# Graph attention on one Trainium2 core: two heads in the halves of a PSUM bank, weight sums in quarters, chunks of 768 columns

## The chip, the core and the metric

The kernel runs on one core of a Trainium2 chip. The metric is the device time of one execution in microseconds (us), and the median of several runs stands for it. One further execution was taken with the hardware profiler, and the parts of the profile come from that one. The engines are PE (TensorE, matrix products), DVE (VectorE), ACT (ScalarE), POOL (GpSimd) and SP (here it only issues DMAs). PSUM is the memory that PE writes its products to[...].

## What is computed

Two layers run on 2708 nodes with 512 features. The change touches only layer 0, an attention over a graph with eight heads of 64 features:

```python
feats = jnp.einsum('nf,hfd->hnd', X, W)
e_self = jnp.einsum('hnd,hd->hn', feats, a_self)
e_neigh = jnp.einsum('hnd,hd->hn', feats, a_neigh)
dense = e_self[:, :, None] + e_neigh[:, None, :]
dense = jnp.where(dense >= 0, dense, LEAKY_ALPHA * dense)
mask = NEG_INF * (1.0 - A)
attn = jax.nn.softmax(dense + mask[None, :, :], axis=-1)
out = jnp.einsum('hnm,hmd->hnd', attn, feats) + b[:, None, :]
```

Here A is the adjacency matrix of zeros and ones, X the normalised and clipped input. The result goes through a relu and is added to the input. Layer 1 (a diffusion with two steps and a nucleus cut) uses A too, in the form A plus the identity and its row and column sums.

## The kernel before

The exponential of a leaky relu is the larger of two products, so an attention weight, up to a factor of its own row, is max(r, k) times A times exp(e_neigh). The factor r belongs to the attending node, k to the neighbour. So the kernel never forms the softmax: DVE computes e = max(r_b, kk) * a_c in one instruction (line 455), and PE multiplies it with `fw`, the features times exp(e_neigh) (line 457). `fw` holds 65 columns for each head: 64 features, and one column with exp(e_neigh) alone, whose product is the sum of the weights. The division by this sum comes at the end.

All this is done in fp32. The 2708 nodes make 22 row tiles: 21 of 128 rows and one of 20. The neighbours lie on the partitions (index `t`), the attending nodes on the columns. The columns are cut into six chunks, four of 512, one of 384 and one of 276 (`tchunks`, line 213). For each chunk:

- Lines 431 to 444: for every row tile `t`, SP loads the chunk's piece of the transposed adjacency, `a_c` (24 buffers of 512 fp32 columns). ACT copies it to `s_c`, summing as it goes; POOL adds the identity on the diagonal; SP stores it to `s_d` for layer 1.
- Line 446, `row_sums`: SP loads 128 whole rows of the adjacency into `arow` (one buffer) and ACT sums them.
- Line 343, `shares`: r is loaded, the same on all partitions, for four heads at a time (`r_b`).
- Lines 449 to 462: the eight heads come in two groups of four. A group has four PSUM accumulators `po`, one bank each out of six, with 65 partitions used. For each of 22 row tiles and each of four heads there are one DVE product e (ten buffers) and one matmul. After the last row tile ACT copies the four accumulators to `o_t` (line 462).
- `finished` (line 351) gives the last part for each row tile of a finished chunk as five stages: `turned` transposes `o_t` on PE; `shared` divides by the sums; `normed` and `cleared` do layer 1's normalisation; `asked` makes transposes and a projection for layer 1. They are put into `later` and are issued, one stage at a time, between the row tiles of the next chunk's first group. Those of the last chunk are issued after its loop.

The order of the instructions on each engine is the program's order as the tile framework lays it out; waits are made by semaphores from the buffers' readers and writers. Layer 1 begins at line 476 and takes the larger part of the time.

Of the kernel before, what the change touches and what calls it, by code (L numbers as in the profile page):

```python
# [9 lines left out]
F32 = mybir.dt.float32  # L10
# [14 lines left out]
P = 128  # L25
# [28 lines left out]
def kernel(  # L54
# [154 lines left out]
    HG = 4  # L209
    hgroups = [list(range(g, min(g + HG, H))) for g in range(0, H, HG)]  # L210

    NB = -(-NT // TG)
    tchunks = []
    for c in range(NB):
        t0 = tchunks[-1][-1] + 1 if c else 0
        tchunks.append(list(range(t0, t0 + NT // NB + (c < NT % NB))))
    with ExitStack() as l0:
        big = l0.enter_context(tc.tile_pool(name="l0", bufs=1))
        fw = big.tile([P, NT, H, DV], F32, name="fw")
# [114 lines left out]

        def row_sums(t):
            pr = rows[t]
            arow = adjp.tile([P, N], F32, name="arow", bufs=1)
            nc.sync.dma_start(out=arow[:pr], in_=adj[cols[t], :])
            nc.scalar.activation(arow[:pr], arow[:pr], AF.Copy, accum_out=rsum[:pr, t:t + 1])
            nc.gpsimd.tensor_scalar(lone[:pr, t:t + 1], rsum[:pr, t:t + 1], 0.0, None, op0=OP.is_equal)  # L340
            nc.gpsimd.tensor_scalar(lone_n[:pr, t:t + 1], lone[:pr, t:t + 1], float(N), None, op0=OP.mult)

        def shares(grp, n0, cw):
            r_b = rbp.tile([P, HG, 512], F32, name="r_b")
# [6 lines left out]
        def finished(t, o_t, c0, bank, final):  # L351


            pr = rows[t]
            f3 = fsum.rearrange("p (h d) -> p h d", h=H)
            pns, held = [], []

            def turned():
                xt = work.tile([P, D], F32, name="xt0", bufs=3)
                nc.sync.dma_start(out=xt[:pr], in_=x[cols[t], :])  # L360
                held.append(xt)
                for g, grp in enumerate(hgroups):
                    pn = bank(g)
                    pns.append(pn[:, :HG * DV].rearrange("p (h d) -> p h d", h=HG))
                    for i, hd in enumerate(grp):
                        nc.tensor.transpose(pns[g][:pr, i, :], o_t[:, hd, c0:c0 + pr], ident[:DV, :DV])

            def shared():
                den = small.tile([P, H], F32, name="den")
                rden = small.tile([P, H], F32, name="rden")  # L370
                o = work.tile([P, D], F32, name="o", bufs=3)
                held.append(o)
                o3 = o.rearrange("p (h d) -> p h d", h=H)
                for pn, grp in zip(pns, hgroups):
                    nc.vector.tensor_scalar(den[:pr, grp[0]:grp[-1] + 1], pn[:pr, :, DH],
                                            lone_n[:pr, t:t + 1], None, op0=OP.add)
                nc.vector.reciprocal(rden[:pr], den[:pr])
                for pn, grp in zip(pns, hgroups):
                    s = slice(grp[0], grp[-1] + 1)
                    nc.vector.scalar_tensor_tensor(o3[:pr, s, :], f3[:pr, s, :], lone[:pr, t:t + 1],  # L380
                                                   pn[:pr, :, :DH], op0=OP.mult, op1=OP.add)
# [12 lines left out]

            def with_beta(o):
                xt = held[0]
                nc.gpsimd.tensor_add(xt[:pr], o[:pr], beta_b[:pr])
                nc.gpsimd.dma_start(out=xb_d[cols[t], :], in_=xt[:pr])

            def cleared():  # L400
                _, o, mean, rs = held
                v = turn.tile([P, D], F32, name="v")
                held.append(v)
                nc.vector.tensor_scalar(o[:pr], o[:pr], mean, rs, op0=OP.subtract, op1=OP.mult)
                nc.scalar.activation(v[:pr], o[:pr], AF.Relu)
# [20 lines left out]
        for ci, tiles in enumerate(tchunks):  # L426
# [3 lines left out]
            a_c = []  # L430
            for t in range(NT):
                pr = rows[t]
                a_c.append(adjp.tile([P, 512], F32, name="a_c", bufs=NT + 2))
                nc.sync.dma_start(out=a_c[t][:pr, :cw], in_=adj_t[cols[t], n0:n1])
                s_c = small.tile([P, 512], F32R, name="s_c", bufs=4)
                wide = len(tiles) * P
                if pr < P or cw < wide:
                    nc.gpsimd.memset(s_c.bitcast(F32), 0.0)
                nc.scalar.activation(s_c[:pr, :cw], a_c[t][:pr, :cw], AF.Copy,  # L439
                                     accum_out=cpart[:pr, t, ci:ci + 1])  # L440
# [7 lines left out]
            o_t = work.tile([DV, H, 512], F32, name="o_t", bufs=1)  # L448
            for grp, r_b in zip(hgroups, r_bs):
                po = [ps_o.tile([P, 512], F32, name="po")[:DV] for _ in grp]  # L450
                for t in range(NT):
                    pr = rows[t]
                    for i, hd in enumerate(grp):
                        e = tp.tile([P, 512], F32, name="e")
                        nc.vector.scalar_tensor_tensor(e[:pr, :cw], r_b[:pr, i, :cw], kk[:pr, t, hd:hd + 1],  # L455
                                                       a_c[t][:pr, :cw], op0=OP.max, op1=OP.mult)
                        nc.tensor.matmul(po[i][:, :cw], lhsT=fw[:pr, t, hd, :], rhs=e[:pr, :cw],  # L457
                                         start=(t == 0), stop=(t == NT - 1))
                    for stage in later.pop(t, ()):
                        stage()  # L460
                for i, hd in enumerate(grp):
                    nc.scalar.copy(o_t[:, hd, :cw], po[i][:, :cw])

            final = ci == len(tchunks) - 1
            for i, t in enumerate(tiles):
                if final:
                    bank = lambda g: ps_o.tile([P, 512], F32, name="po")
                else:
                    bank = lambda g: ps_t.tile([P, 512], F32, name=f"pn{g}")
                for n, stage in enumerate(finished(t, o_t, t * P - n0, bank, final)):  # L470
# [983 lines left out]
```

## Time and profile before

| what | value |
|---|---|
| median of three runs | 3573.36 us (3570.47 to 3583.9) |
| profiled execution, its own time | 3562.47 us |
| span of the profile | 3560.7 us |
| mean granted clock of PE | 0.976 |
| first and last matmul of line 457 begin | 138.6 us, 1044.2 us |
| PE, DVE, ACT, POOL busy, of the whole span | 94%, 74%, 42%, 25% |

A group line of the profile names the source line, the engine, the operation, what is written and read, the shape and the number of instructions; then the busy time and the mean of one in ns; then the idle time of the engine just before, and what ended it. PEld is PE's loading of the weights, which can run beside the matmuls. Durations of matmuls include the time in the pipeline, so they overlap in the trace; the distance from one weight load to the next shows the real pace. An answer for one line says how long its engine was idle before it, how many times, and until what.

### The profile page before, as it was taken

What the parts mean: (1) busy time and instruction counts of PE and PEld (TensorE: products, weight loads), DVE (VectorE), ACT (ScalarE), POOL (GpSimd) and SP (SyncE); (2) the same over time, 40 slices, a digit from 0 to 9 for tenths busy, and PEclk for the clock granted to TensorE, in tenths of its full rate; (3) what the DMA queues carried; (4) which work ended last, traced back from release to release, by engine and by line L of the source; (5) the groups of instructions that cost most, each with busy time, mean ns of one, the idle gap of its engine ahead of it and who ended that gap; (6) DMA issues with size and microseconds to landing.
All of it is one profiled execution on the core that took longest, in us unless ns stands there. A gap on an engine that the chain in (4) does not pass through costs nothing. (4 is left out here: it accounts for less than half of the span.)

```text
span 3560.7 us, 34129 instructions
## 1 busy us (share of the span) xinstructions
PE 3332.0 (94%) x10797; PEld 1729.1 (49%) x10797; DVE 2650.8 (74%) x4828; ACT 1508.6 (42%) x2269; POOL 890.4 (25%) x1074
## 2 busy tenths in 40 slices
PE   8999999998988999999999999899998999988998
PEld 4433333333455544646555554465555555555554
DVE  4587888889985756545464734598899998888883
ACT  2344211111103676566565642353655554545610
POOL 4114241415321121211222221311312332212211
PEclk9999999999999999999999999999999999999999
DMA  4476424242327624525344453695545535556453
GB/s 116 155 244 243 154 95 139 76 125 84 103 98 269 238 83 153 196 90 208 108 157 170 136 175 101 226 307 169 175 163 189 199 130 183 174 183 210 163 202 124
DMA packets 251348, 579.99 MB, mean 163 GB/s; under 512 B 33945, under 2 KB 76553, under 8 KB 248291
## 3 DMA queue, kind: packets, MB, share of 16 engines
q1 hardware_dynamic: 229063, 503.39, 42.7%
q0 software_dynamic: 22064, 74.09, 5.4%
q8 instruction: 86, 1.41, 0.2%
q14 instruction: 135, 1.11, 0.1%
HBM read 471.68 MB, written 105.68 MB: 162 GB/s over the span
## 5 line engine op out<-in xcount | busy, mean ns | idle before, releaser
L1140 PE MATMUL a<-va,at 128*128 128x512 f32 (+2 forms) x1936 | 887.1, 598 | 5.0 <-ACT at L1122 4.7
L457 PE MATMUL po<-e,fw 128*65 128x512 f32 (+4 forms) x2112 | 841.9, 554 | 28.8 <-DVE e L455 20.4
L455 DVE SCALAR_TENSOR_TENSOR e<-r_b,kk,a_c 128x512 f32<-128x512 f32 (+4 forms) x1056 | 750.4, 739 | 70.0 <-PE po L457 19.0
L576 ACT ACTIVATE junk_a<-p,nth 128x2708 uint8<-128x2708 f32 (+1 forms) x240 | 612.8, 2553 | 32.1 <-POOL nth L591 27.6
L1014 PE MATMUL q<-hl,s_r 128*128 128x512 f32 x1936 | 537.9, 424 | 63.3 <-DMA s_r<-s_d 45.3
L457 PEld LDWEIGHTS po<-e,fw 128*65 128x65 f32 (+1 forms) x2112 | 287.3, 140 | 543.5 <-issue 275.1
L1140 PEld LDWEIGHTS a<-va,at 128*128 128x128 f32 (+2 forms) x1936 | 338.3, 186 | 374.5 <-issue 341.9
L1014 PEld LDWEIGHTS q<-hl,s_r 128*128 128x128 f32 x1936 | 363.5, 192 | 225.9 <-issue 64.8
L1122 ACT COPY at<-t 128x512 f32<-128x512 f32 (+3 forms) x308 | 140.6, 478 | 655.8 <-PE t L1118 652.4
L655 DVE SCALAR_TENSOR_TENSOR junk<-p,th 128x2708 bf16<-128x2708 f32 (+1 forms) x132 | 407.2, 3085 | 3.0
L1034 PE MATMUL q<-u_k,v 128*128 128x512 f32 x704 | 316.9, 592 | 0.8 <-ACT v L1024 0.8
L1017 PE MATMUL q<-s_r,hl 128*128 128x512 f32 (+1 forms) x1056 | 282.3, 413 | 15.2 <-DMA s_r<-s_d 11.1
L1017 PEld LDWEIGHTS q<-s_r,hl 128*128 128x128 f32 x1056 | 196.0, 192 | 94.9 <-issue 51.6
L1034 PEld LDWEIGHTS q<-u_k,v 128*128 128x128 f32 x704 | 133.3, 190 | 158.6 <-issue 154.4
L544 ACT COPY p<-t 128x452 f32<-128x452 f32 (+2 forms) x264 | 131.3, 536 | 162.0 <-PE t L542 115.6
L542 PE MATMUL t<-keys,q_t 128*128 128x452 f32 x528 | 160.9, 432 | 41.2 <-ACT p L544 38.1
L851 DVE MAX8 vn<-keep 128x8 f32<-128x2708 f32 (+1 forms) x66 | 196.8, 2981 | 2.3
L569 DVE TENSOR_REDUCE nmx<-p 128x1 f32<-128x2708 f32 (+1 forms) x44 | 130.5, 2967 | 88.1 <-ACT p L544 88.1
L439 ACT ACTIVATE s_c<-a_c 128x512 fp32r<-128x512 f32 (+3 forms) x132 | 76.2, 577 | 249.0 <-DMA a_c<-in_adj_t_dram 122.3
L1187 PE MATMUL a<-u_k,v_t 128*128 128x512 f32 (+1 forms) x352 | 168.6, 619 | 5.2 <-ACT yo L1194 3.0
L1118 PEld LDWEIGHTS t<-ident,keep 128*128 128x128 f32 (+1 forms) x968 | 114.7, 139 | 76.1 <-issue 46.5
L1118 PE MATMUL t<-ident,keep 128*128 128x128 f32 (+1 forms) x968 | 145.3, 272 | 2.9 <-ACT p L544 2.8
(311 smaller groups left out, 3358.2 us busy)
## 6 DMA issues: line engine op xcount, KB each, us to landing
hl<-vhl_d SPq DMA_DIRECT2D x132, 512.0 KB
s_r<-s_d SPq DMA_DIRECT2D x264, 256.0 KB
hl<-fhl_d SPq DMA_DIRECT2D x132, 512.0 KB
hl<-bhl_d SPq DMA_DIRECT2D x132, 512.0 KB
u_k<-in_L_gnn_U_dram SPq DMA_DIRECT2D x184, 256.0 KB
arow<-in_adj_dram SPq DMA_DIRECT2D x21, 1354.0 KB
s_r<-s_d SPq DMA_DIRECT2D x132, 192.0 KB
s_d<-s_c SPq DMA_DIRECT2D x88, 256.0 KB
```

Source lines behind the costliest of these rows:

```text
L455: nc.vector.scalar_tensor_tensor(e[:pr, :cw], r_b[:pr, i, :cw], kk[:pr, t, hd:hd + 1], a_c[t][:pr, :cw], op0=OP.max, op1=OP.mult)
L457: nc.tensor.matmul(po[i][:, :cw], lhsT=fw[:pr, t, hd, :], rhs=e[:pr, :cw], start=(t == 0), stop=(t == NT - 1))
L542: nc.tensor.matmul(pl[:, :c1 - c0], lhsT=q[:, i], rhs=self.keys[:, c0:c1], start=(i == 0), stop=(i == 1))
L576: nc.scalar.activation(junk[:pr], self.p[i][:pr], func, **kw)
L655: nc.vector.scalar_tensor_tensor(self.junk_b[:pr], p, th, p, op0=OP.is_ge, op1=OP.mult, accum_out=dst)
L851: v.max(vs, keep[0][:pr])
L1014: nc.tensor.matmul(half[j], lhsT=s_r[:, j * P:(j + 1) * P], rhs=hl[:, h], start=(c == 0 and h == 0), stop=(c == NT - 1 and h == 1))
L1017: nc.tensor.matmul(half[j][:, :w], lhsT=hl[:, h, j * P:(j + 1) * P], rhs=s_r[:, :w], start=(c == 0 and h == 0), stop=(c == NT - 1 and h == 1))
L1034: nc.tensor.matmul(half[j], lhsT=across_t[-1][k][:, j * P:(j + 1) * P], rhs=u_k, start=(start and k == 0), stop=(start and k == KD - 1))
L1118: nc.tensor.transpose(pt[:rows[c], j, :pr], keep[i][:pr, cols[c]], ident[:pr, :pr])
L1140: nc.tensor.matmul(pa[:pr], lhsT=at[:rows[c], j, :pr], rhs=va[:rows[c], c, :], start=(c == 0), stop=(c == NT - 1))
L1187: nc.tensor.matmul(pz[i][:rows[t]], lhsT=v_t[i][:, k, :rows[t]], rhs=u_k, start=(k == 0), stop=(k == KD - 1))
```

## The change

The accumulators no longer have 65 partitions. Two heads share one bank: head i of a pair has partitions 0 to 63 or 64 to 127, so each matmul has 64 weight columns. The sums of the weights get banks of their own: four heads in four quarters of 32 partitions, where the one column with exp(e_neigh) is read 32 times (`to_broadcast`). Three kinds of accumulator (two pairs, one of sums) by two parts of at most 512 columns take six banks, so a chunk has 768 columns: three chunks of 768 and one of 404 instead of six. A chunk of 768 is streamed to PE in two parts of 384.

To make room, the adjacency is loaded into `a_f` (three fp32 buffers) and ACT casts it to `a_c` in bf16 (zeros and ones stay exact); `s_c` has three buffers instead of four; `arow` holds half a row; e has six buffers of 768 columns instead of ten of 512. `o_t` holds two heads on its 128 partitions, `o_d` the sums; a row tile then takes six transposes instead of eight. The stages in `later` are placed anew.

```diff
-    NB = -(-NT // TG)
-    tchunks = []
...
+    TC = 6
+    WC = TC * P
+    tchunks = [list(range(t, min(t + TC, NT))) for t in range(0, NT, TC)]
+    NG = len(hgroups)
+    NPR = HG // 2
...
-        tp = l0.enter_context(tc.tile_pool(name="l0t", bufs=10))
+        tp = l0.enter_context(tc.tile_pool(name="l0t", bufs=6))
...
-            arow = adjp.tile([P, N], F32, name="arow", bufs=1)
-            nc.sync.dma_start(out=arow[:pr], in_=adj[cols[t], :])
-            nc.scalar.activation(arow[:pr], arow[:pr], AF.Copy, accum_out=rsum[:pr, t:t + 1])
+            half = small.tile([P, 2], F32, name="half")
+            w = -(-N // 2)
+            for i in range(2):
+                arow = adjp.tile([P, w], F32, name="arow", bufs=1)
+                c = slice(i * w, min((i + 1) * w, N))
+                arow = arow[:pr, :c.stop - c.start]
+                nc.sync.dma_start(out=arow, in_=adj[cols[t], c])
+                nc.scalar.activation(arow, arow, AF.Copy, accum_out=half[:pr, i:i + 1])
+            nc.gpsimd.tensor_tensor(rsum[:pr, t:t + 1], half[:pr, 0:1], half[:pr, 1:2], op=OP.add)
...
-                a_c.append(adjp.tile([P, 512], F32, name="a_c", bufs=NT + 2))
-                nc.sync.dma_start(out=a_c[t][:pr, :cw], in_=adj_t[cols[t], n0:n1])
-                s_c = small.tile([P, 512], F32R, name="s_c", bufs=4)
+                a_f = adjp.tile([P, WC], F32, name="a_f", bufs=3)
+                nc.sync.dma_start(out=a_f[:pr, :cw], in_=adj_t[cols[t], n0:n1])
+                a_c.append(adjp.tile([P, WC], BF16, name="a_c", bufs=NT + 2))
+                nc.scalar.copy(a_c[t][:pr, :cw], a_f[:pr, :cw])
+                s_c = small.tile([P, WC], F32R, name="s_c", bufs=3)
...
-            for grp, r_b in zip(hgroups, r_bs):
-                po = [ps_o.tile([P, 512], F32, name="po")[:DV] for _ in grp]
+            halfs = -(-cw // 512)
+            hw = -(-cw // halfs)
+            parts = [(a, min(a + hw, cw)) for a in range(0, cw, hw)]
+            for gi, (grp, r_b) in enumerate(zip(hgroups, r_bs)):
+                po = [[ps_o.tile([P, 512], F32, name="po") for _ in parts] for _ in range(NPR + 1)]
                 for t in range(NT):
                     pr = rows[t]
-                    for i, hd in enumerate(grp):
-                        e = tp.tile([P, 512], F32, name="e")
-                        nc.vector.scalar_tensor_tensor(e[:pr, :cw], r_b[:pr, i, :cw], kk[:pr, t, hd:hd + 1],
-                                                       a_c[t][:pr, :cw], op0=OP.max, op1=OP.mult)
-                        nc.tensor.matmul(po[i][:, :cw], lhsT=fw[:pr, t, hd, :], rhs=e[:pr, :cw],
-                                         start=(t == 0), stop=(t == NT - 1))
-                    for stage in later.pop(t, ()):
+                    es = []
+                    for k in range(NPR):
+                        for i in (2 * k, 2 * k + 1):
+                            hd = grp[i]
+                            e = tp.tile([P, WC], F32, name="e")
+                            es.append(e)
+                            nc.vector.scalar_tensor_tensor(e[:pr, :cw], r_b[:pr, i, :cw], kk[:pr, t, hd:hd + 1],
+                                                           a_c[t][:pr, :cw], op0=OP.max, op1=OP.mult)
+                        for n, (a, b) in enumerate(parts):
+                            for i in range(2):
+                                nc.tensor.matmul(po[k][n][i * DH:(i + 1) * DH, :b - a],
+                                                 lhsT=fw[:pr, t, grp[2 * k + i], :DH], rhs=es[2 * k + i][:pr, a:b],
+                                                 start=(t == 0), stop=(t == NT - 1))
+                    w = P // HG
+                    for n, (a, b) in enumerate(parts):
+                        for i, hd in enumerate(grp):
+                            nc.tensor.matmul(po[NPR][n][i * w:(i + 1) * w, :b - a],
+                                             lhsT=fw[:pr, t, hd, DH:].to_broadcast([pr, w]), rhs=es[i][:pr, a:b],
+                                             start=(t == 0), stop=(t == NT - 1))
+                    for stage in later.pop(gi * NT + t, ()):
                         stage()
-                for i, hd in enumerate(grp):
-                    nc.scalar.copy(o_t[:, hd, :cw], po[i][:, :cw])
+                for k in range(NPR + 1):
+                    for n, (a, b) in enumerate(parts):
+                        to = o_t[:, gi * NPR + k, a:b] if k < NPR else o_d[:, gi, a:b]
+                        nc.scalar.copy(to, po[k][n][:, :b - a])
...
-                if final:
+                if final and i < 3:
...
-                    later.setdefault(n if final else i * 5 + n, []).append(stage)
+                    later.setdefault(n if final else 3 * i + n + n // 4, []).append(stage)
```

More of the change, by code (lines that the diff above doesn't have):

```diff
@@ L210 @@
     hgroups = [list(range(g, min(g + HG, H))) for g in range(0, H, HG)]
-    NB = -(-NT // TG)
-    tchunks = []
-    for c in range(NB):
-        t0 = tchunks[-1][-1] + 1 if c else 0
-        tchunks.append(list(range(t0, t0 + NT // NB + (c < NT % NB))))
+    TC = 6
[3 more added lines that the diff above has]
+    NPR = HG // 2
     with ExitStack() as l0:
@@ L343, in shares @@
         def shares(grp, n0, cw):
-            r_b = rbp.tile([P, HG, 512], F32, name="r_b")
+            r_b = rbp.tile([P, HG, WC], F32, name="r_b")
             nc.sync.dma_start(
@@ L349, in shares, with finished @@
             return r_b
-        def finished(t, o_t, c0, bank, final):
+        def finished(t, o_t, o_d, c0, bank, final):
             pr = rows[t]
-            f3 = fsum.rearrange("p (h d) -> p h d", h=H)
             pns, held = [], []
@@ L361, in turned @@
                 held.append(xt)
-                for g, grp in enumerate(hgroups):
-                    pn = bank(g)
-                    pns.append(pn[:, :HG * DV].rearrange("p (h d) -> p h d", h=HG))
-                    for i, hd in enumerate(grp):
-                        nc.tensor.transpose(pns[g][:pr, i, :], o_t[:, hd, c0:c0 + pr], ident[:DV, :DV])
+                for g, (src, n) in enumerate(((o_t, H // 2), (o_d, NG))):
+                    pns.append(bank(g).rearrange("p (k d) -> p k d", k=KD))
+                    for k in range(n):
+                        nc.tensor.transpose(pns[g][:pr, k, :], src[:, k, c0:c0 + pr], ident)
             def shared():
@@ L373, in shared @@
                 o3 = o.rearrange("p (h d) -> p h d", h=H)
-                for pn, grp in zip(pns, hgroups):
-                    nc.vector.tensor_scalar(den[:pr, grp[0]:grp[-1] + 1], pn[:pr, :, DH],
-                                            lone_n[:pr, t:t + 1], None, op0=OP.add)
+                pn, pd = pns
+                nc.vector.tensor_scalar(den[:pr], pd[:pr, :NG, ::P // HG].rearrange("p g i -> p (g i)"),
+                                        lone_n[:pr, t:t + 1], None, op0=OP.add)
                 nc.vector.reciprocal(rden[:pr], den[:pr])
[L378 to L381, printed above, removed]
+                nc.vector.scalar_tensor_tensor(o[:pr], fsum[:pr], lone[:pr, t:t + 1],
+                                               pn[:pr].rearrange("p k d -> p (k d)"), op0=OP.mult, op1=OP.add)
                 eng = nc.vector if final else nc.gpsimd
@@ L438 @@
                     nc.gpsimd.memset(s_c.bitcast(F32), 0.0)
-                nc.scalar.activation(s_c[:pr, :cw], a_c[t][:pr, :cw], AF.Copy,
+                nc.scalar.activation(s_c[:pr, :cw], a_f[:pr, :cw], AF.Copy,
                                      accum_out=cpart[:pr, t, ci:ci + 1])
@@ L447 @@
             r_bs += [shares(grp, n0, cw) for grp in hgroups[1:]]
-            o_t = work.tile([DV, H, 512], F32, name="o_t", bufs=1)
-            for grp, r_b in zip(hgroups, r_bs):
-                po = [ps_o.tile([P, 512], F32, name="po")[:DV] for _ in grp]
+            o_t = work.tile([P, H // 2, WC], F32, name="o_t", bufs=1)
+            o_d = work.tile([P, NG, WC], F32, name="o_d", bufs=1)
+            halfs = -(-cw // 512)
+            hw = -(-cw // halfs)
+            parts = [(a, min(a + hw, cw)) for a in range(0, cw, hw)]
@@ L460 @@
+                    w = P // HG
[5 more added lines that the diff above has]
+                    for stage in later.pop(gi * NT + t, ()):
                         stage()
-                for i, hd in enumerate(grp):
-                    nc.scalar.copy(o_t[:, hd, :cw], po[i][:, :cw])
+                for k in range(NPR + 1):
+                    for n, (a, b) in enumerate(parts):
+                        to = o_t[:, gi * NPR + k, a:b] if k < NPR else o_d[:, gi, a:b]
+                        nc.scalar.copy(to, po[k][n][:, :b - a])
@@ L469 @@
                     bank = lambda g: ps_t.tile([P, 512], F32, name=f"pn{g}")
-                for n, stage in enumerate(finished(t, o_t, t * P - n0, bank, final)):
-                    later.setdefault(n if final else i * 5 + n, []).append(stage)
+                for n, stage in enumerate(finished(t, o_t, o_d, t * P - n0, bank, final)):
+                    later.setdefault(n if final else 3 * i + n + n // 4, []).append(stage)
         for n in sorted(later):
```

## The prediction

> **What bounds the kernel now.** The change touches only the graph attention of layer 0, so I first find that stretch. In the page's forty slices PE, the matmul engine, is at 8 or 9 tenths nearly throughout. The table of groups then gives the loop's two instructions, the answer for line 457 and the wait table of the stretch from 138 to 1050 us say who waits for whom:
>
> ```profile
> L457 PE MATMUL po<-e,fw 128*65 128x512 f32 (+4 forms) x2112 | 841.9, 554 | 28.8 <-DVE e L455 20.4
> L455 DVE SCALAR_TENSOR_TENSOR e<-r_b,kk,a_c 128x512 f32<-128x512 f32 (+4 forms) x1056 | 750.4, 739 | 70.0 <-PE po L457 19.0
> ```
> ```profile
>   DVE e L455: 230.9, 636
>   ACT o_t L462: 23.6, 13
> ```
> ```profile
> DVE e L455 <- PE po L457: 19.0, 31, 6.0
> ```
>
> The reader sees 1056 products e on DVE (VectorE) and twice as many matmuls: every fp32 matmul is two instructions. The second fence is the answer for line 457, what PE and its weight loads waited for (us, times): at the ends of groups ACT's copies out of PSUM, 23.6 us in all; the 230.9 on e are mostly loads that arrive early and lie under the matmul before. The third is the wait table: DVE waits for PE 31 times. Line 457 runs from 138.6 to 1044.2 us: 905.6 us. Who sets its pace is read from the timeline of PE's weight loads at the switch from 128 to 20 rows:
>
> ```profile
> 212.37 0.14 PEld L457 LDWEIGHTS po<-e,fw 128*65 128x65 f32 x1 [0.29 <-issue]
> 213.31 0.19 PEld L457 LDWEIGHTS po<-e,fw 20*65 20x65 f32 x2 [0.81 <-DVE e L455]
> 213.80 0.13 PEld L457 LDWEIGHTS po<-e,fw 20*65 20x65 f32 x1 [0.30 <-issue]
> 214.23 0.13 PEld L457 LDWEIGHTS po<-e,fw 20*65 20x65 f32 x1 [0.30 <-issue]
> ```
>
> In steady state a load comes every 0.43 us and hides under the matmul before it: 0.429 us for 512 columns, 0.838 ns a column and instruction. Here the same three loads take 1.43 us instead of 1.29: **a switch of array mode costs 0.14 us**, and its first load is not pulled ahead. Streaming alone is 1408 x 0.429 (512 columns) + 352 x 0.322 (384) + 352 x 0.231 (276) = 798 us, 108 short of the stretch. So PE bounds the stage. DVE is next: the table of six windows, 138 to 1050 us, sums to
>
> ```profile
> sum 912.00, PE 873.84 PEld 327.82 DVE 810.17 ACT 195.66 POOL 270.54; mean PE 145.64 PEld 54.64 DVE 135.03 ACT 32.61 POOL 45.09
> ```
>
> DVE's 810 us are 750 of e and some 60 of the later stages.
>
> **What the Trainium skill says.** "FP8 and Floating Point Precision", TensorE Precision Notes: true fp32 takes four passes. The trace agrees in kind: two instructions for each matmul of line 457; it doesn't show the passes within one. "TensorE: Matmul & The Clock Gate", Part 3: small matmuls in different column strips of the array run at once (three of 32 columns: 2.38x), but matmuls start and end in program order. No matmul of the trace before pairs strips, so it shows neither. "TensorEngine Tiling (Array Packing)", Key Properties: a change of tiling mode drains the array; the 0.14 us above agrees. "VectorE: DVE Perf Modes", What auto-detection actually checks: the two-per-cycle form of a two-input operation wants every tensor 16 bits wide. Only a_c becomes bf16 while r_b and e stay fp32, so I give DVE nothing for the type; no run here shows it.
>
> **The change part by part.**
>
> *DVE.* 1056 products become 704: 528 of 768 columns and 176 of 404. In this stretch the means are 793 ns (512), 700 (384), 567 (276): 0.96 ns a column. So 768 take 793 + 256 x 0.96 = 1.04 us, 404 take 0.69, together 549 + 121 = 670 us, 80 less than now. DVE isn't the bound, so by itself this is worth nothing.
>
> *PE.* For one group of four heads and one row tile of 768 columns, PE now streams 8 x 768 x 0.838 ns = 5.15 us. After, two pairs in halves, two parts of 384 columns: 8 matmuls; the sums in quarters: 8 more. That is 32 instructions of 0.322 us, and two mode switches (64 to 32 columns and back), 0.28. The time depends on what overlaps. I take this rule: a strip's instruction starts when its own strip is free and none ahead of it still waits. Each head's two instructions share a strip, so the second waits for the first and holds up the next head. The halves then overlap two deep (8 slots of 0.322 for 16 instructions, plus one to fill), but the quarters also only two deep: 8 slots plus one. 18 x 0.322 + 0.28 = **6.08 us** against 5.15. For 404 columns (one part): 10 x 0.339 + 0.28 = 3.67. With 2 x 22 x 3 = 132 of the first and 44 of the second: 803 + 161 = **964 us** of streaming, for 798.
>
> *Buffers.* e falls from ten of 512 to six of 768, and all four e of a row tile are held until the sums have read them. DVE can be only two products ahead. Under the rule above e0 is free some 1.3 us before the sums end, so the third and fourth products are ready in time. Where the quarters overlap four deep, it bites (below).
>
> *The rest of the stage.* The 108 us are: waits at group ends 24; 176 transposes of o_t (8 in 1.07 us: 0.13 each) 23; the later stages' transposes and projections (228 x 0.12) 27; 24 row switches 3; waits for e and small things 31. After: eight ends instead of twelve, each with six copies of 0.47 us instead of four, and all six banks in use instead of four of six; but the first banks finish while the sums still run, so 16 us. 132 transposes 16. The others stay at 61. Say 95.
>
> *Costed at nothing, and the cover.* ACT: 88 casts of some 0.85 us (the 512-column s_c took 0.63) and 88 s_c for 132, about 60 us more beside 196 busy of 912. They lie between a load and the first product, so the first chunk begins some 2 us later; if ACT's queue is blocked, PE's start of each chunk slips. SP: 176 adjacency loads and stores for 264, and 44 half rows for 22, bytes unchanged; a_f has three buffers, held by ACT for some 1.9 us a row tile against 6 us of PE. DMA moved 270 GB/s in the first 162 us, so it has slack while a chunk takes longer. The last chunk finishes four tiles instead of three: 3 us, beside layer 1's first matmuls. DVE's den and o operations are halved in number: off the path.
>
> *The sum.* 964 + 95 = 1059 us for 905.6: **+153**. The profiled execution took 3562.5 us (span 3560.7 and 1.8 around it), so 3716. The median of the three runs, 3573.4, is 11 above; I take 3715, the median's excess being within the sum's error.
>
> **The unknown costs, both ends.** Switch of column mode: not in the trace; from nothing to twice the row switch, 0 to 98 us over 352 switches; I take 0.14 (49). Overlap: from none to full, in the rivals. Fill slots: nothing to one each; without fill and switch the streaming is again 798. The likeliest case's own range is therefore 3580 to 3790.
>
> **The rivals.**
>
> *Full overlap, held by e* (0.22). If each strip has its own queue, the quarters take 4 slots: 12 slots + 0.28 = 4.14 us. Then all e come free together at the end. Third and fourth product need 2.1 us more, the second pair runs from 2.2 to 3.5, sums end at 4.92, next tile at 5.06; for 404 columns 3.12. 132 x 5.06 + 44 x 3.12 = 805, + 95 = 900: 3568; 3545 to 3610 with DVE's 60 us of other work partly in that loop. For: no run here shows that a held-up strip holds up the others. Against: the skill's program order.
>
> *Full overlap and DVE as the bound* (0.12; the other side). If e comes free early enough, DVE runs through: 670 + 60 + 30 of starts and ends = 760, **-145: 3430**. It decides from the point where a 768-column tile takes under 5.2 us, since (132 + 44 x 0.61) x T + 95 falls below 905 there. Against: six buffers.
>
> *No overlap, the strips only named* (0.18): the change doesn't do what it says. 32 x 0.322 + 0.28 = 10.6 us and 5.7: 1397 + 251 + 95 = 1743, **+837: 4410**. For: nothing in this trace shows two fp32 matmuls at once.
>
> *Halves overlap, quarters don't* (0.08): 25 slots, 8.33 and 4.69 us: 1401, +495: 4070.
>
> **How the numbers follow.** In order held up (0.40) 3715; the rivals as given. The range goes from 3430, the DVE-bound case, to 4080, past the fourth rival; the unoverlapped case (0.18) stays out. Half a per cent is 18 us, about what a measurement of this kernel can tell from no change. Faster: the DVE-bound case and a fifth of the first rival, 0.16; same: most of that rival, 0.12; slower: 0.72.
>
> **What would show it.** The pace of the weight loads in the new loop: 32 loads in 6.1 us per 768-column tile is the forecast, 5.1 the first rival, 10.6 no overlap. Matmuls of two halves starting within some 0.32 us of each other; of four quarters, in steps of 0.32 (forecast) or together (rivals). A gap of about 0.14 at each change of width. e of 768 columns near 1.04 us; DVE's share of the stage down from 89% to about 70%. Wrong if the first matmul of a chunk waits long for a cast, or if DVE is the one that never idles.

## The result, and the profile after

The median of seven runs went from 3579.24 us (3570.47 to 3583.9) to 3588.76 us (3584.77 to 3599.71): ratio 1.0039, 95% interval 1.0020 to 1.0057. The change costs 0.4%, where the forecast, 3715, had it cost 4%. The first rival, "full overlap, held by e", had 3568 in a range of 3545 to 3610.

The profiled execution has a span of 3583.0 us, at a mean granted clock of 0.976 as before. In the changed kernel line 467 is the product e, line 471 the feature matmuls in halves, line 477 the sums in quarters, line 485 the copies out of PSUM. The page's table of groups:

```profile
L467 DVE SCALAR_TENSOR_TENSOR e<-r_b,kk,a_c 128x768 f32<-128x768 f32 (+3 forms) x704 | 671.4, 1008 | 161.1 <-PE po L477 154.4
...
L471 PE MATMUL po<-e,fw 128*64 128x384 f32 (+3 forms) x2464 | 583.9, 516 | 21.2 <-DVE e L467 20.4
```

DVE is busy with the products for 671.4 us, before for 750.4. But it now stands idle for 154.4 us until the sums, line 477, have been read out of e; before, it was 19.0. The table of waits, 138 to 1060 us, shows both directions (us, times, longest):

```profile
PEld po L471 <- DVE e L467: 162.6, 277, 6.4
DVE e L467 <- PE po L477: 154.4, 128, 3.2
```

PE's weight loads wait for e, and DVE waits for PE to give e back: a loop through the buffers. The first line alone doesn't show it, since a load that waits can lie under the matmul before it, as with the 230.9 us of the prediction's second fence; the idle time that the page gives PE for e is 20.4 us before and after. What it costs is read from the pace of the loads and from the experiments. DVE's share of the stretch from 138 to 1050 us is 726.78 of 912.00, 80%:

```profile
sum 912.00, PE 894.01 PEld 299.36 DVE 726.78 ACT 244.78 POOL 296.34; mean PE 894.01 PEld 299.36 DVE 726.78 ACT 244.78 POOL 296.34
```

What PE does is read from the timeline of its weight loads (start, duration, and at the end of the line the idle time before):

```profile
642.44 0.16 PEld L477 LDWEIGHTS po<-e,fw 128*32 128x32 f32 x8 [0.60 <-issue]
642.79 0.13 PEld L477 LDWEIGHTS po<-e,fw 128*32 128x32 f32 x4 [0.19 <-issue]
643.11 0.13 PEld L477 LDWEIGHTS po<-e,fw 128*32 128x32 f32 x4 [0.19 <-issue]
643.86 0.20 PEld L471 LDWEIGHTS po<-e,fw 128*64 128x64 f32 x4 [0.62 <-DVE e L467]
644.24 0.15 PEld L471 LDWEIGHTS po<-e,fw 128*64 128x64 f32 x2 [0.17 <-issue]
644.56 0.15 PEld L471 LDWEIGHTS po<-e,fw 128*64 128x64 f32 x2 [0.17 <-issue]
645.31 0.14 PEld L477 LDWEIGHTS po<-e,fw 128*32 128x32 f32 x2 [0.60 <-issue]
646.07 0.19 PEld L471 LDWEIGHTS po<-e,fw 128*64 128x64 f32 x2 [0.62 <-DVE e L467]
646.73 0.20 PEld L471 LDWEIGHTS po<-e,fw 128*64 128x64 f32 x4 [0.47 <-DVE e L467]
```

Loads of the quarters come in **fours** every 0.32 us, those of the halves in twos (the first count of a block is larger: loads for the next slot are pulled ahead). The prediction had asked whether the matmuls of four quarters start in steps of 0.32 us or together. It is together: the first four of this block start within 0.02 us. The block of 16 sums instructions lasts from 642.44 to 643.86, 1.42 us: four slots of 0.322 and 0.13 for the change of width. The last three lines are the loop through the buffers: PE has the first pair done, one sums matmul (two instructions) is put in between, and the second pair comes in pieces, as DVE delivers e.

**Where the time went.** From the first feature matmul at 140.3 to the last sums matmul at 1045.8 the stage takes 905.5 us, where it took 905.6. The two figures agree by chance: they are two different bounds. The extra time lies at the end. From the stage's end to the first matmul of layer 1's `a` product, called the hand-off below, the kernel before takes 157.5 us, the changed one 172.8. The timeline of SP shows where it sticks:

```profile
1048.95 0.42 SPq L1032 DMA_DIRECT2D s_r<-s_d  x1
1060.70 0.31 SPq L365 DMA_DIRECT2D xt<-in_x_dram  x1
```

Line 365 loads the input rows `xt` for a finished row tile. The last chunk now finishes four row tiles at once, `xt0` has three buffers, so the fourth load waits until one is free, and the next loads for layer 1, the following `s_r` among them, stand behind it on SP. In the timeline of PE, two holes follow:

```profile
1053.73 4.84 PE L1040 MATMUL q<-s_r,hl 128*128 128x512 f32 x20 [0.59 <-DVE o L382]
1069.10 3.75 PE L1040 MATMUL q<-s_r,hl 128*128 128x512 f32 x8 [10.53 <-DMA s_r<-s_d]
...
1095.69 1.90 PE L175 MATMUL t<-v_t,kw 128*128 128x20 f32 x8 [9.65 <-ACT v_t L164]
```

10.53 us until the rows `s_r` have landed, and 9.65 us for the 20-row tile's `v_t`. Of the span's 22.3 us, 15.3 are this hand-off and 1.7 the later start of the stage; the remaining 5 or so lie in layer 1, whose second step varied between profiled executions by more than that.

### The profile page after: what moved, and what is told of

Same layout as the page of the kernel before. It is cut to its first block, busy times and chain, and to the rows that moved or that the text cites. A ratio compares the mean times of both kernels' runs of the same rounds, so it can differ in the third digit from the quotient of the medians.

```text
span 3583.0 us, 39468 instructions
## 1 busy us (share of the span) xinstructions
PE 3353.9 (94%) x13569; PEld 1700.8 (47%) x13569; DVE 2578.9 (72%) x4436; ACT 1559.3 (44%) x2307; POOL 929.1 (26%) x1091
## 5 line engine op out<-in xcount | busy, mean ns | idle before, releaser
L467 DVE SCALAR_TENSOR_TENSOR e<-r_b,kk,a_c 128x768 f32<-128x768 f32 (+3 forms) x704 | 671.4, 1008 | 161.1 <-PE po L477 154.4
L471 PE MATMUL po<-e,fw 128*64 128x384 f32 (+3 forms) x2464 | 583.9, 516 | 21.2 <-DVE e L467 20.4
L471 PEld LDWEIGHTS po<-e,fw 128*64 128x64 f32 (+1 forms) x2464 | 189.3, 138 | 375.7 <-issue 186.4
L477 PE MATMUL po<-e,fw 128*32 128x384 f32 (+3 forms) x2464 | 295.0, 500 | 0.0
L477 PEld LDWEIGHTS po<-e,fw 128*32 128x32 f32 (+1 forms) x2464 | 70.3, 108 | 201.7 <-issue 201.3
L154 POOL TENSOR_SCALAR ln_rs<-ln_mv 128x1 f32<-128x1 f32 x66 | 47.8, 725 | 421.3 <-DVE ln_mv L153 420.4
```

What stands on the lines that cost most here:

```text
L471: nc.tensor.matmul(po[k][n][i * DH:(i + 1) * DH, :b - a], lhsT=fw[:pr, t, grp[2 * k + i], :DH], rhs=es[2 * k + i][:pr, a:b], start=(t == 0 ...
L477: nc.tensor.matmul(po[NPR][n][i * w:(i + 1) * w, :b - a], lhsT=fw[:pr, t, hd, DH:].to_broadcast([pr, w]), rhs=es[i][:pr, a:b], start=(t == ...
```

## The experiments

Theory A, formed on reading the trace: the strips of the array run fully beside each other, and the six buffers of e hold the loop. Rival B, the forecast's rule: quarters run only two deep. Rival C: the pace is set by the switches of width, of which the trace shows 482 where 352 were written, since the order that the framework lays out puts single sums matmuls ahead of a tile's second pair. A stage's length is from the first feature matmul to the last sums matmul. Edits are against the changed kernel. Ratios are to runs of the kernel before on the same chip.

### Room alone, and two more buffers of e

More buffers of e need room. In `ctl` the row sums are loaded in quarters and `a_c` loses its two spare buffers; `e8` is the same with eight buffers of e.

```diff
 ctl:
-            half = small.tile([P, 2], F32, name="half")
-            w = -(-N // 2)
-            for i in range(2):
+            half = small.tile([P, 4], F32, name="half")
+            w = -(-N // 4)
+            for i in range(4):
...
-                a_c.append(adjp.tile([P, WC], BF16, name="a_c", bufs=NT + 2))
+                a_c.append(adjp.tile([P, WC], BF16, name="a_c", bufs=NT + 0))
 e8, besides:
-        tp = l0.enter_context(tc.tile_pool(name="l0t", bufs=6))
+        tp = l0.enter_context(tc.tile_pool(name="l0t", bufs=8))
```

> The changed kernel with room made in SBUF and nothing else: the rows for the row sums are loaded in quarters instead of halves (88 loads for 44), and the cast adjacency a_c has 22 buffers instead of 24. It is the control for the run with eight buffers of e. Both theories (e's buffers hold the loop; PE's own pace holds it) expect no change against the changed kernel, 3588 us within 8; a third, that the casts and the prefetch across chunks hold it, expects some 10 to 40 us more.

> As the control, but e has eight buffers of 768 columns instead of six, so that DVE can make all four products of the next row tile while PE works on this one. Theory: PE overlaps fully (12 slots of 0.322 and two switches, 4.14 us a row tile of 768 columns) and waits for the third and fourth product, which have no buffer until the sums have read the first two. Then a row tile falls from 5.06 to some 4.4 us (DVE's four products 4.2 and its other work), 404 columns from 3.1 to 2.8: 132 x 0.66 + 44 x 0.3 = 100 us less than the control, 3490, between 3460 and 3510. Rival: PE's own pace (switches, loads of weights, program order) sets the 5 us; then no change, 3588 within 8.

`ctl`: 3592.26 us, ratio 1.0053 (1.0032 to 1.0075), stage 905.3 us: the room costs the stage nothing. `e8`: 3506.20 us, ratio 0.9807 (0.9790 to 0.9824), stage 823.4 us. **Two more buffers take 82 us out of the stage**, where A had 100. The table of waits of `e8`, 138 to 1040 us (its lines stand one lower):

```profile
DVE e L468 <- PE po L478: 61.6, 67, 7.5
```

DVE's wait for the sums goes from 154 to 62 us, somewhat more than the stage shortens. So e's buffers held the loop.

### Two fewer buffers of e

```diff
-        tp = l0.enter_context(tc.tile_pool(name="l0t", bufs=6))
+        tp = l0.enter_context(tc.tile_pool(name="l0t", bufs=4))
```

> The changed kernel with four buffers of e instead of six and nothing else. Theory (e's buffers hold the loop, PE overlaps fully): no product of the next row tile can be made before the sums have read this one's, so the first pair waits 2.1 us and the second to 4.3: 4.3 + 1.29 + 0.14 + 1.29 + 0.14 = 7.1 us a row tile of 768 columns and 4.6 of 404; 132 x 2.0 + 44 x 1.5 = 330 us more, the stage 1235 us long instead of 906, the whole 3920. Rival (PE's own pace): PE is busy 5 us a row tile and hides at least half of it; 0 to 100 us more.

3788.35 us in one run, stage 1100 us: 194 more, where A had 330 and its rival at most 100. The direction is A's, the size is not. The timeline of DVE:

```profile
600.34 3.81 DVE L467 SCALAR_TENSOR_TENSOR e<-r_b,kk,a_c 128x768 f32<-128x768 f32 x4 [3.54 <-PE po L477]
606.91 3.81 DVE L467 SCALAR_TENSOR_TENSOR e<-r_b,kk,a_c 128x768 f32<-128x768 f32 x4 [2.76 <-PE po L477]
```

With four buffers DVE makes four products and stops until the sums are through: 3.81 + 2.76 = 6.57 us for a row tile. Here a product takes 0.95 us, where the mean in the changed kernel is 1.096. With that, four products take 3.81 us and not 4.3, and the expected period of 7.1 us was too long.

### No strip beside another

All heads of a row tile go into the same half and the same quarter, which alternate from tile to tile; the same number of matmuls of the same size.

```diff
-                                nc.tensor.matmul(po[k][n][i * DH:(i + 1) * DH, :b - a],
+                                nc.tensor.matmul(po[k][n][t % 2 * DH:(t % 2 + 1) * DH, :b - a],
...
-                            nc.tensor.matmul(po[NPR][n][i * w:(i + 1) * w, :b - a],
+                            nc.tensor.matmul(po[NPR][n][t % 4 * w:(t % 4 + 1) * w, :b - a],
```

(The start and stop flags follow, and the divisor in `shared` is kept at 1 or above.)

> The changed kernel with no two neighbouring matmuls in different strips: within a row tile both heads of a pair go to the same half (even tiles the first, odd the second), and all four sums to the same quarter, so features and sums of heads are added up in wrong places; the number, widths and durations of the instructions, the loads and the switches stay. It measures what the overlap is worth. Theory (strips overlap fully): 32 slots instead of 12, 10.6 us a row tile for 5.06, and 5.7 for 3.1 at 404 columns: 132 x 5.5 + 44 x 2.6 = 840 us more, 4430, between 4380 and 4480. Rival (halves two deep and quarters only two deep, as was predicted): the same 4430, but then the changed kernel's own pace would have been 6.1 and not 5.1. Rival (no overlap in the changed kernel): no change, 3590.

Stage 1773 us in one run, 867 more, at a granted clock of 0.97 in the stage, in the changed kernel 0.98. Only the stage is read: layer 1's work depends on the values that it gets, and these are other ones. The timeline of weight loads shows single loads where the changed kernel has pairs and fours:

```profile
1001.23 0.14 PEld L471 LDWEIGHTS po<-e,fw 128*64 128x64 f32 x1 [0.19 <-issue]
1001.55 0.14 PEld L471 LDWEIGHTS po<-e,fw 128*64 128x64 f32 x1 [0.18 <-issue]
```

One instruction every 0.32 us, as the prediction's case without overlap had it (1743 us for the stage). So what the strips bring is 867 us, and the choice of the output's partitions alone decides whether they bring it.

### Quarters two deep

The sums of four heads go into two of the four quarters, odd row tiles into the other two: B's pace by construction.

```diff
-                            nc.tensor.matmul(po[NPR][n][i * w:(i + 1) * w, :b - a],
+                            nc.tensor.matmul(po[NPR][n][(i % 2 + t % 2 * 2) * w:(i % 2 + t % 2 * 2 + 1) * w, :b - a],
```

> The changed kernel with the sums of four heads in two quarters instead of four (heads 0 and 2 in one, 1 and 3 in the next; the other two quarters on odd row tiles), so sums are added up in wrong places and the time after this stage means nothing: only the stage is read. This is how deep the forecast thought that the quarters overlap. Theory (quarters run four deep in the changed kernel): the sums now take 8 slots of 0.322 for 4, but their first two e come free 0.64 us before the end, so the second pair waits less: 5.7 us a row tile for 5.06, 3.0 for 3.1 at 404 columns, the stage 80 us longer, 985, between 960 and 1010. Rival (the forecast's rule, that four quarters already run only two deep): no change, 906.

Stage 1004 us in one run, 99 more, at a granted clock of 0.97, and the loads of line 477 come in twos:

```profile
641.64 0.12 PEld L477 LDWEIGHTS po<-e,fw 128*32 128x32 f32 x2 [0.21 <-issue]
641.96 0.12 PEld L477 LDWEIGHTS po<-e,fw 128*32 128x32 f32 x2 [0.21 <-issue]
```

If B's rule held, this edit would have changed nothing; A's expectation was 985, between 960 and 1010. **B falls.** Even so the stage isn't at the forecast's 1059: in the same timeline the block of sums lasts from 641.29 to 644.00, 2.71 us, which is eight slots and a switch and leaves none for a slot to fill.

### The order written out

`o6` is the changed kernel with PE's order in the chunk loop fixed as the program writes it; `o8` is `e8` with the same.

```diff
-        for ci, tiles in enumerate(tchunks):
+        with tc.manual_schedule(engines={PE}):
+            for ci, tiles in enumerate(tchunks):
```

> The changed kernel with PE's instructions in this stage in the order in which the loops are written (a manual schedule for PE). In the changed kernel's trace PE's order is another: in some 65 of 176 row tiles a single matmul of the sums stands between the first and the second pair, with two more switches of width, 482 switches in all instead of 352. Theory (e's buffers hold the loop): these singles lie in time in which the second pair waits for its products anyway, so no change to 15 us less: 3575 to 3592. Rival (switches and order set PE's pace): 65 x 0.7 = 45 us less, 3545.

> Eight buffers of e (room made as in the control) and PE in the loops' order. Theory: with eight buffers the second pair's products are there, so a single matmul of the sums pulled ahead now costs PE its two switches and the lost overlap, some 0.7 us; 36 of them make 25 us, less what DVE's work of 730 us in a stage of 823 leaves open: 10 to 25 us less than the run with eight buffers, 3480 to 3497. Rival (a denser PE lowers the granted clock, as the run with ten buffers seems to show): no gain or a loss, 3505 to 3540, with a mean clock below 0.97.

`o6`: 3605.98 us, ratio 1.0086 (1.0060 to 1.0113), stage 910.2 us. The switches fall from 482 to 352, and the stage doesn't gain, where C had 45 us less: the singles pulled ahead lie in time that PE would wait anyway. C falls. `o8`: 3492.64 us, ratio 0.9762 (0.9735 to 0.9788), stage 811.3: where e no longer holds the loop, the same edit takes 12 us off the stage. In all `o6` lies some 17 us above the changed kernel and outside what was expected. Its stage has 5 of them; between the two profiled executions all else that is clearly longer comes after layer 1's first step (see "Left open" below).

### Ten buffers, and the blocked evacuation

For ten buffers of e, `s_c` is merged into `a_f`, which is summed and stored in place and has four buffers; the rest as `e8`. `o10` is this with PE's order written out.

```diff
-        tp = l0.enter_context(tc.tile_pool(name="l0t", bufs=6))
+        tp = l0.enter_context(tc.tile_pool(name="l0t", bufs=10))
...
-                nc.scalar.activation(s_c[:pr, :cw], a_f[:pr, :cw], AF.Copy,
+                nc.scalar.activation(a_f[:pr, :cw], a_f[:pr, :cw], AF.Copy,
```

> The same room, all of it for e: ten buffers of 768 columns. Theory: with eight, DVE (some 730 us of work in a stage of 823) and PE (some 745) still wait for each other in turn, because DVE has four free buffers only when the sums end; with ten it can start two products earlier and the stage comes down to DVE's work and the starts and ends, 780 to 800: 3465 to 3485. Rival: with eight the loop is already at DVE's pace and only its other work lengthens it; then 3500 to 3510, as with eight.

> Ten buffers of e (room made as in the earlier run with ten) and PE in the loops' order. The earlier run with ten was slower than with eight at a lower granted clock. Theory of the clock (the more of PE's time runs several strips at once, the lower the clock): still lower than 0.963, and 3530 to 3570. Rival (the loss with ten came from the order that the scheduler chose, not from the clock): back at eight's time or better, 3470 to 3505, clock near 0.972.

Both missed. `e10`: 3539.55 us, ratio 0.9885 (0.9853 to 0.9916), stage 848.5; `o10`: 3524.26, ratio 0.9845 (0.9816 to 0.9873), stage 834. Both are slower than with eight buffers. The room isn't why: `e8x4`, below, has the same room with eight, and its stage is 823.6. What grows are two of PE's waits. One is seen in `e10` at the first chunk's end. Its timeline of ACT:

```profile
347.32 0.77 ACT L344 ACTIVATE arow<-arow 128x677 f32<-128x677 f32 x1 [4.04 <-DMA arow<-in_adj_dram]
...
348.08 1.60 ACT L485 COPY o_t<-po 128x384 f32<-128x384 f32 x4
```

Row sums that wait for DMAs run on ACT ahead of the copies out of PSUM, so the six banks (tiles of 128 x 512 fp32 in PSUM) stay full and PE waits 14.6 us. What comes after is seen in the weight loads:

```profile
348.59 0.30 PEld L471 LDWEIGHTS po<-e,fw 128*64 128x64 f32 x4 [15.83 <-ACT o_t L485]
349.29 0.24 PEld L471 LDWEIGHTS po<-e,fw 128*64 128x64 f32 x2 [0.40 <-ACT o_t L485]
349.93 0.24 PEld L471 LDWEIGHTS po<-e,fw 128*64 128x64 f32 x2 [0.40 <-issue]
...
356.23 0.14 PEld L471 LDWEIGHTS po<-e,fw 128*64 128x64 f32 x2 [0.18 <-issue]
356.56 0.14 PEld L471 LDWEIGHTS po<-e,fw 128*64 128x64 f32 x2 [0.18 <-issue]
```

Pairs come every 0.64 us at first and every 0.32 later. The table of windows has the granted clock behind the busy times:

```profile
338.00:348.00 10.00, 0.00 (x0) 0.00 (x0) 0.00 (x0) 3.55 (x9) 0.00 (x0) 0.50 0.82 252
348.00:354.00 6.00, 5.41 (x24) 1.91 (x28) 0.00 (x0) 2.44 (x8) 0.82 (x4) 0.56 0.82 312
354.00:380.00 26.00, 24.59 (x192) 9.80 (x184) 20.61 (x27) 5.79 (x13) 17.10 (x16) 1.00 0.46 128
```

The clock is 0.50 while PE is idle, 0.56 in the next 6 us and 1.00 after. `o10` has the same hole, 14.49 us, before its matmul at 344.06.

The other wait is for `v_t`, which a finished tile's projection (line 175) needs and ACT copies out of PSUM (line 417). The tables of waits have it, first that of `e8` from 138 to 964 us, then that of `e10` from 138 to 989 us:

```profile
PE pn L175 <- ACT v_t L417: 3.3, 2, 1.7
...
PE pn L175 <- ACT v_t L417: 29.6, 11, 3.6
```

In the same tables PE's idle time until the copies out of PSUM (`o_t`) goes from 9.7 to 24.9 us, and until e down from 25.3 to 12.4. Together the three grow by 29 us, where the stage is 25 longer. From `o8` to `o10` the wait for `v_t` goes from 18.0 to 52.6 us, the three together again by 29, where the stage is 23 longer. In the timeline of `e10` one such copy, at 385.77, comes only after ACT has waited 4.30 us for DVE with the next tile's `v`, though PE began the transposes that it copies at 377.94. Why such waits are longer with ten buffers than with eight was not followed up.

The expectation of `o10` had weighed whether denser work of PE lowers the clock. Over the stage the granted clock is 0.93 in `e10` and 0.97 in `e8`. But in the table above it is 1.00 where PE works densely and low where PE had stood still; around the wait at 385.77 it is 0.50 from 384 to 390 us. No run took the waits away at ten buffers, so how much of the 25 us each of them and the low clock make up stays open.

### The hand-off to layer 1

`x4`: the room of `ctl` (one spare `a_c` kept), with a fourth buffer of `xt0` and `o`. `e8x4`: eight buffers of e, the same fourth buffers, and the room of `e10`.

```diff
-                xt = work.tile([P, D], F32, name="xt0", bufs=3)
+                xt = work.tile([P, D], F32, name="xt0", bufs=4)
...
-                o = work.tile([P, D], F32, name="o", bufs=3)
+                o = work.tile([P, D], F32, name="o", bufs=4)
```

> The changed kernel with four buffers instead of three for the input rows xt0 and the outputs o of finished row tiles (room made by row sums in quarters, 23 buffers of a_c). Theory on the 17 us that the changed kernel loses between the layers: its last chunk has four row tiles, the load of the fourth xt0 waits on SP's queue until the first is free, and layer 1's loads stand behind it, so PE idles 10 us for s_r and 10 us more for the last tile's projection. Then 10 to 18 us less than the changed kernel, 3570 to 3580. Rival: the fourth row tile costs this by its own work; then 0 to 4 us less.

> Eight buffers of e and four of xt0 and o, with room made by doing layer 1's copy s_c in place in a_f (four buffers) besides row sums in quarters and 22 buffers of a_c. Theory: as the run with eight buffers, 3506, less the 8 us that four xt0 and o took from the stretch between the layers: 3498, between 3485 and 3510. Rival: a_f, now held until its store, brings waits at the chunks' starts: 3510 to 3540.

`x4`: 3592.24 us, ratio 1.0039 (1.0023 to 1.0054). The wait for `s_r`, 10.5 us in the changed kernel, is 1.6, and a later matmul waits instead. Its line in the timeline:

```profile
1072.73 2.08 PE L175 MATMUL t<-v_t,kw 128*128 128x128 f32 x8 [7.99 <-ACT v_t L164]
```

The hand-off is 165.9 us, against 172.8 and, in `ctl`, 171.9: six or seven of the fifteen come back, the rest goes into waits for `v_t`, the end of the finished tiles' own chain. In the total the expected 10 to 18 us less did not come: `x4` can't be told from `ctl`. `e8x4`: 3508.07 us, ratio 0.9809 (0.9781 to 0.9837), stage 823.6, hand-off 167.1 where `e8` has 175.4; no gain in the total either.

`o8x` puts together what had helped: `o8` with four `xt0` and, for their room, two `s_c`.

```diff
-                xt = work.tile([P, D], F32, name="xt0", bufs=3)
+                xt = work.tile([P, D], F32, name="xt0", bufs=4)
...
-                s_c = small.tile([P, WC], F32R, name="s_c", bufs=3)
+                s_c = small.tile([P, WC], F32R, name="s_c", bufs=2)
```

> The run with eight buffers of e and PE in the loops' order, with four buffers of xt0 instead of three (room: two of s_c instead of three). In that run PE stood 10.5 us after the stage for s_r, whose loads wait on SP's queue behind the fourth row tile's xt0. Theory: this idle time goes and the time falls by 5 to 10 us against 3493: 3480 to 3488, ratio to the kernel before 0.974. Rival: other work stands on that stretch and takes the gain back, as the earlier run with four xt0 suggested (there the first scores of layer 1 came 8 us earlier and the whole time did not fall): 3490 to 3496, ratio 0.976.

3485.03 us (3481.24 to 3489.77), ratio 0.9736 (0.9710 to 0.9762): **the fastest version, 2.6% under the kernel before.** Stage 810.7, hand-off 164.2, in `o8` 811.3 and 175.0. In all it is 7.6 us under `o8`, as expected, but the intervals of the two ratios overlap, so that step is likely, not shown. Its table of windows, 138 to 952 us:

```profile
sum 814.00, PE 765.30 PEld 275.93 DVE 726.19 ACT 257.64 POOL 314.45; mean PE 765.30 PEld 275.93 DVE 726.19 ACT 257.64 POOL 314.45
```

DVE is busy for 726 of 814 us, 89%: the second rival's bound is near, though its 760 us are not reached.

## Why the prediction was wrong

**The step that failed is the overlap of the quarters.** The prediction's rule was that a head's second instruction, waiting for its own strip, holds up the next head; so eight slots for the sums and a slot to fill each width, 6.08 us for a row tile of 768 columns and 964 us of streaming. In the trace the quarters' loads come in fours, and the 16 instructions take four slots and a switch, 1.42 us, where the forecast had nine slots and a switch, 3.04. `two` forces two deep on the quarters and costs 99 us, `strip` takes the overlap away and costs 867. The prediction leaned on "TensorE: Matmul & The Clock Gate", Part 3, that matmuls start and end in program order, and read into it that a matmul waiting for its strip stops those behind it. What this page states of small matmuls in different column strips running at once is what the trace shows, here also for fp32, with four strips and two instructions for each head; that the order holds up other strips, no run here shows. The traces don't tell in which order PE's program has the two instructions of each head, and so not whether any overtakes another; they show that the quarters don't wait for each other. "TensorEngine Tiling (Array Packing)", Key Properties, has that different tiles run matmuls in parallel; the trace agrees.

**The switch of column mode** was taken as 0.14 us with no line for it: 0.13 at the sums block. This term was right in size. Only the number of switches was not foreseen, 482 for 352, and `o6` shows that with six buffers of e the others cost the stage nothing.

**The buffers.** Under the failed rule, six buffers of e would have been enough; under full overlap the first rival had them hold the loop at 5.06 us for a row tile. An estimate: taking the prediction's 95 us for the rest of the stage, which were not measured apart, from 905.5, and 0.62 tiles for one of 404 columns, leaves 810 / (132 + 44 x 0.62) = 5.09 us; the rival's stage of 900 us was within 6. Its total was 5 us less than before, where 10 more were measured; the longer hand-off, 15.3 us, makes up the difference. In the same way `e8` comes to 4.6 and `o8x` to 4.5 us, towards the 4.14 that PE alone would take. The prediction's own formula gives 5.1 us, and not 5.2, as the tile's time below which the stage gets shorter; with 5.09 the changed kernel happens to stand on that line. That e is the cause is shown by both directions, `e8` with 82 us less and `e4` with 194 more.

**DVE.** The forecast's 670 us and the 671.4 measured agree by luck. The 670 add up means, and the sum of the measured durations is 704 x 1.008 = 710 us (before, 1056 x 0.739 = 780); the 671.4 are busy time, which counts overlapping products once. One of 768 columns takes 1.096 us on the mean and not 1.04. No gain by the bf16 adjacency is seen, as taken. DVE's share is 80% and not 70, since the stage didn't get longer.

**ACT's casts and the later start.** Forecast about 2 us, measured 1.7 (138.6 to 140.3). In the changed kernel's table of waits DVE waited for a cast once, 5.9 us.

**The end of the last chunk** was mis-sized: 3 us beside layer 1 were forecast, the hand-off is 15.3 us longer. The fourth finished tile was counted as work of PE; its load as a step on SP's queue, ahead of layer 1's loads and with three buffers for four tiles, was not. With a fourth `xt0`, in `x4` together with a fourth `o` and in `o8x` alone, the 10.5 us wait for `s_r` is 1.6, and `v_t` is late next.

**Left open:** what of the total's differences of 5 to 20 us arises in layer 1. Its second step, from the last matmul of the first step's `a` product to its own, took 1286 us before, 1291 after, 1306 in `ctl`, 1309 in `x4` and 1312 in `o6`, each in one profiled execution. The stretch between the two steps' `a` products alone took 163 us after and 172 or 173 in `ctl`, `o6` and `o10`, at a granted clock of 0.96 and of 0.92 to 0.93. So why the shorter hand-off of `x4` doesn't show in the total stays open too.

## What to carry to other kernels

Count the array's slots for each strip, not for each instruction: here fp32 matmuls put side by side in column strips took 867 us less than one after the other. Then count how long each operand buffer is held by its last reader; here the reader that came last in the row tile, the sums, kept all four e, and PE lost 82 us of the stage for want of two buffers. When a stage issues one more load than its buffers hold, look at what stands behind it on that queue.

## What the runs showed of the hardware

- Four quarters of 32 columns run at full depth with two instructions for each fp32 matmul: 16 instructions of 384 columns in 1.42 us, a switch of width included; in one strip at a time each takes 0.32 us.
- A change of width between 64 and 32 columns costs 0.13 us in the trace, the same as a change of rows before.
- After 14.6 us of idle PE the matmuls ran at half pace for some 5 us: pairs of loads every 0.64 us for 0.32; the granted clock was 0.50 in the wait and 0.56 in the 6 us after it. The Trainium skill, "TensorE: Matmul & The Clock Gate", Part 1, states a half clock after idling; the trace agrees. Such a wait here cost more than its length.
- More buffers made the kernel slower than fewer, 3539.55 us with ten of e and 3506.20 with eight, and the traces show PE waiting longer for ACT: 24.9 us for 9.7 until copies out of PSUM, where row sums that wait for their loads run ahead of them, and 29.6 for 3.3 until `v_t`.
